# Queries and keys of chunk pairs by Strassen's seven products, in an attention block

## The chip, the cores and the metric

The kernel runs on one core of one Trainium2 chip. The metric is the device time of one execution in microseconds. The time before the change is the median of three runs, 2641.21 us (2639.83 to 2642.91).

## The reference, cut to what matters

Four sequences of 1024 tokens by 512 features are normalized (`xn`). A block of attention with 16 heads of 128 and a small product in rounded FP8 are added to the input. What the change touches is the first part: queries and local keys are products of the same tokens with two weights, and each head of them is divided by its root mean square, weighted, and rotated in its first 64 columns.

```python
q  = apply_rope(rmsnorm((xn @ Wq  + bq ).reshape(..., 16, 128), qn_w), pos)
lk = apply_rope(rmsnorm((xn @ Wlk + blk).reshape(..., 16, 128), kn_w), pos)
lv = (xn @ Wlv + blv)
# local: each chunk of 128 tokens sees itself and the chunk before it
# sparse: the 8 best of the compressed entries ck (one for 4 tokens), with values cv
out = x + ((ctx_sparse + ctx_local) * 0.5) @ Wo + bo + fp8(xn) @ fp8(input2)
```

All of it is in float32, apart from the FP8 part.

## The kernel before

The 4096 tokens are cut into 32 chunks of 128 (`t`), eight for each sequence. The 16 heads are cut into eight units of two heads (`u`). A unit of a chunk is the piece of work `n = 8 t + u`, 256 of them. One loop over slots `s` from -3 to 252 (its end is written out separately) issues, in an order written out by hand, the stages of several units: the scores of unit `s`, the queries of unit `s + 3`, the values of unit `s - 1`, the output of unit `s - 2`. No scheduler moves an instruction: each engine works through its own queue in the order of the source, and waits where data or a buffer isn't ready. All DMAs of the loop go through the SP queue, in that order too.

The stages of one unit, with the lines of the profile:

- `queries` (L606): four matmuls of 128x512 into the PSUM tile `qp` (two buffers). The 512 columns are 256 of `Wq` and 256 of `Wlk`, both heads. In chunks after the first, the first of the four inputs is `xone`, a copy of the tokens with a row of ones in it, since the bias stands in the weight's row 0.
- `squares`, `spread` (L321, L315, L316): ScalarE sums the squares of each head, GpSimd takes the power -1/2.
- `normalize` (L634): VectorE reads `qp` in PSUM and writes `th` in SBUF, four operations of 128x128. GpSimd makes one product of the rotation (L337), VectorE the other (L339, into `thb`, which is then still free) and the two sums (L341, L342).
- `turn_keys` (L687, L690, L695): VectorE transposes blocks of 32 into `thb` (one buffer), and four DMAs carry it to DRAM (`qk`). `fetch_keys` (L705) brings it back transposed as `qT` and `lkT`, two DMAs. It is called for unit `s + 2` right after the fetch of the weights in slot `s`.
- `scores` (L754, L761, L764) into `sc` (PSUM, one buffer); `weigh` (L786 to L822): VectorE masks, finds the maximum (L786) and the eight best (L807, L812), and negates the latter (L809), ScalarE takes exponentials; `settle` (L830 to L840): VectorE keeps the eight best, guards the sum (L839) and takes the reciprocal; `divide` (L847): ScalarE, four operations.
- `turn`, `fetch` (L865, L873, L907): the weights go through DRAM too: VectorE transposes blocks, one DMA writes `pr`, four read `probT`.
- `values_of` (L712): local values, four matmuls of 128x256. `values` (L924), `keep_context` (L939), `to_output` (L957): the context and its product with `wo`. All eight units' `wo` lie in SBUF for the whole run.

Beside the units, generators prepare a chunk (`chunk_prep`, `chunk_entries`, `chunk_eight`): layer norm, pooling, the FP8 part. Their steps are called at fixed units of a chunk. Their DMAs are the stores of the transposed tokens (L1091), `fetch_tokens` (L491, into `xnT`, two buffers), `fetch_with_ones` (L503), the loads of x (L105) and of angles (L111), and now and then the pooled entries (L527).

Of the order around the change, this is the heart (in slot `s`):

```python
for_unit(s, (scores, 0), (scores, 1))
for_unit(s, (weigh,))
for_unit(s + 3, (queries,))
for_unit(s + 2, (normalize,))
for_unit(s, (settle,)); for_unit(s, (divide,))
for_unit(s + 2, (go_on_rotating,), (end_rotation,))
turn(s); for_unit(s + 2, (turn_keys,))
for_unit(s - 2, (to_output,)); for_unit(s + 1, (values_of,)); for_unit(s - 1, (values,))
fetch(s); for_unit(s + 2, (fetch_keys,))
# then stores, tokens, ones and loads
```

Of the kernel before, what the change touches and what calls it, by code (L numbers as in the profile page):

```python
# [19 lines left out]
P = 128  # L20
D = 128
# [17 lines left out]
def kernel(  # L39
# [34 lines left out]
    NN = NT * NU  # L74
    assert S // RATIO <= 2 * P and NU == 8 and HID == 512
# [10 lines left out]
    def scratch(name, shape=(P, 512), dtype=F32):  # L86
        return work.tile(list(shape), dtype, tag="scratch", name=name, bufs=2)

# [19 lines left out]
    def load_angles(t):  # L108
        c = t % NCH
        cs = work.tile([P, ROPE], F32, tag="cs", name=f"cs_{t}")  # L110
        nc.sync.dma_start(cs, rope[ts(c, P), :])  # L111
        angles[t] = cs
# [10 lines left out]
    wqk_sb = [const.tile([P, KK, 512], F32, name=f"wqk_{u}") for u in range(NU)]  # L123
    wlv_sb = [const.tile([P, KK, 256], F32, name=f"wlv_{u}") for u in range(NU)]
    wo_sb = [const.tile([P, 2, HID], F32, name=f"wo_{u}") for u in range(NU)]

    def load_wqk(u, engine):
        for i, w in enumerate((Wq, Wlk)):
            engine.dma_start(
                wqk_sb[u][:, :, ts(i, 256)], w[:, ts(u, 256)].rearrange("(k p) n -> p k n", p=P)  # L130
            )
# [4 lines left out]
    def load_wo(u, engine):  # L136
        engine.dma_start(wo_sb[u], Wo[ts(u, 256), :].rearrange("(h p) n -> p h n", p=P))
# [13 lines left out]
    for k in range(KK):  # L151
        for i, w in enumerate((Wq, Wlk)):
            nc.sync.dma_start(wqk_sb[0][:, k, ts(i, 256)], w[ts(k, P), 0:256])
# [28 lines left out]
    bias_b = const.tile([P, 512], BF16, name="bias_b")  # L182
# [80 lines left out]
    def fold_first_row(u):  # L263
        w = wqk_sb[u]
        row = first_row.pop(u, None)
        if row is None:
# [3 lines left out]
                row, ident[:, 0:1].to_broadcast([P, P]), w[:, 0, :], start=True, stop=True  # L270
            )
        nc.vector.tensor_tensor(
            w, w, row.unsqueeze(1).to_broadcast([P, KK, 512]), ALU.subtract
        )
        for i, bias in enumerate((bq, blk)):
            nc.sync.dma_start(
                w[0:1, 0, ts(i, 256)], bias[ts(u, 256)].partition_broadcast(1)
            )

# [24 lines left out]
    w2_raw = [wo_sb[NU // 2 + k][:, 0, :] for k in range(KK)]  # L304

    def round_w2():
        for k in range(KK):
            spare = wo_sb[NU // 2 + k][:, 1, :]
# [14 lines left out]
    def rotate(th, cs, nh, a, name, bb=None):  # L323
# [17 lines left out]
        nc.vector.tensor_tensor(x12[:, :, 0, :], a[:, :, 0, :], bb[:, :, 1, :], ALU.subtract)  # L341
        nc.vector.tensor_tensor(x12[:, :, 1, :], a[:, :, 1, :], bb[:, :, 0, :], ALU.add)  # L342
# [135 lines left out]
    def turn_tokens_here(xt):  # L478
# [4 lines left out]
        xnT = work.tile([P, KK, P], F32, tag="xnT", name="xnT_0")  # L483
# [3 lines left out]
    def fetch_tokens(t):  # L487
        xnT = work.tile([P, KK, P], F32, tag="xnT", name=f"xnT_{t}")
# [5 lines left out]
        chunks[t] = xnT, xones[t % 2]  # L494


    xones = [const.tile([P, P], F32, name=f"xone_{i}") for i in range(2)]

    def fetch_with_ones(t):
        turned = tokens.pop(t).rearrange("i (b k) a j -> b i k (a j)", b=NB)  # L500
        for b in range(NB):
            lo = 0 if b else 1
            nc.sync.dma_start(  # L503
                xones[t % 2][b * BLK + lo : (b + 1) * BLK], turned[b, lo:, 0, :]
# [96 lines left out]
    def queries(n):  # L601
        t, u = place(n)
        xnT, xone = chunks[t]
        qp = psum.tile([P, 512], F32, tag="qp", name=f"qp_{n}")
        for k in range(KK):
            nc.tensor.matmul(  # L606
                qp,
                xnT[:, k, :] if k or not t else xone,
                wqk_sb[u][:, k, :],
# [7 lines left out]
        ss = work.tile([P, 4], F32, tag="ss", name=f"ss_{n}")  # L617
        units[n] = {"qp": qp, "ss": ss}

    def squares(n, heads):  # L620
        w = units[n]
        for i in heads:
            square_sum(w["ss"][:, i : i + 1], w["qp"][:, ts(i, D)], f"{n}_{i}")
# [5 lines left out]
    def normalize(n):  # L629
        w = units[n]  # L630
        qp, r = w.pop("qp"), w["r"]
        th = work.tile([P, 4, D], F32, tag="th", name=f"th_{n}", bufs=1)
        for i in range(4):
            nc.vector.scalar_tensor_tensor(  # L634
                th[:, i, :],
                qp[:, ts(i, D)],
# [9 lines left out]
        w["th"], w["thb"] = th, thb  # L646
# [27 lines left out]
    def key_tiles(n):  # L674
        w = units[n]
        qT = work.tile([P, NB, 2 * BLK], F32, tag="qT", name=f"qT_{n}", bufs=2)
        lkT = work.tile([P, NB, 2 * BLK], F32, tag="lkT", name=f"lkT_{n}", bufs=NU + 2)
# [3 lines left out]
    def turn_keys(n):  # L681
# [11 lines left out]
        turned = dram.tile([NB, NB, BLK, 4 * BLK], F32, tag="qk", name=f"qk_{n}")  # L693
# [43 lines left out]
    def scores(n, h):  # L737
# [6 lines left out]
        if n == NN - 2:  # L744

            w.setdefault("sc", []).append(psum.tile([P, 512], F32, tag="qp", name=f"sc_{n}_{h}"))
# [19 lines left out]
    def weigh(n):  # L766
# [5 lines left out]
            [  # L772
# [443 lines left out]
```

## Time and profile before

| what | value |
|---|---|
| median of three runs | 2641.21 us |
| profiled execution, from its first to its last instruction | 2641.7 us |
| granted TensorE clock | 0.999 |
| DMA: moved, share of 16 engines' time on the queue of the loop | 422.20 MB, 58.8% |
| qp<-wqk, L606, 128x512 float32: all 2048 instructions, busy | 968.1 us |
| vp<-wlv, L712, 128x256 float32: 2048 instructions, busy | 483.6 us |
| op<-wo, L957, 128x512 float32: 1024 instructions, busy | 481.6 us |

The profile gives each engine's busy time (PE is TensorE's matmuls, PEld its weight loads, DVE VectorE, ACT ScalarE, POOL GpSimd, SPq the SP queue that issues DMAs). A group's line has the source line, engine, operation, output and inputs, shape and count, then the busy time and the mean duration of one. Each float32 matmul call appears as two instructions. The mean duration of a matmul (593 ns at 512 columns) is longer than the time from one to the next, because they overlap in the pipeline.

### The profile page before, as it was taken

What the parts mean: (1) busy time and instruction counts of PE and PEld (TensorE: products, weight loads), DVE (VectorE), ACT (ScalarE), POOL (GpSimd) and SP (SyncE); (2) the same over time, 40 slices, a digit from 0 to 9 for tenths busy, and PEclk for the clock granted to TensorE, in tenths of its full rate; (3) what the DMA queues carried; (4) which work ended last, traced back from release to release, by engine and by line L of the source; (5) the groups of instructions that cost most, each with busy time, mean ns of one, the idle gap of its engine ahead of it and who ended that gap; (6) DMA issues with size and microseconds to landing.
All of it is one profiled execution on the core that took longest, in us unless ns stands there. A gap on an engine that the chain in (4) does not pass through costs nothing.

```text
span 2641.7 us, 46868 instructions
## 1 busy us (share of the span) xinstructions
PE 2609.3 (99%) x11879; PEld 1784.3 (68%) x11879; DVE 2213.4 (84%) x8381; ACT 1390.9 (53%) x5560; POOL 786.2 (30%) x1128
## 2 busy tenths in 40 slices
PE   8999999999999999999999999999999999999998
PEld 4666666776666666767766666667666666676776
DVE  6888888889888888888888888888888888877886
ACT  3545545555555555555555555555555555555555
POOL 3522323223332223232233322233323322322222
PEclk9999999999999999999999999999999999999999
DMA  8356556666655555666655555666665555566554
GB/s 255 110 156 162 151 145 175 171 176 158 164 143 154 162 155 156 169 173 170 166 157 144 158 149 158 177 164 164 171 176 147 150 148 153 147 168 171 159 152 110
DMA packets 722252, 422.20 MB, mean 160 GB/s; under 512 B 395823, under 2 KB 671552, under 8 KB 721984
## 3 DMA queue, kind: packets, MB, share of 16 engines
q1 hardware_dynamic: 721952, 419.20, 58.8%
q8 instruction: 97, 1.59, 0.3%
q14 instruction: 171, 1.40, 0.2%
q10 hardware_dynamic: 32, 0.02, 0.0%
HBM read 225.80 MB, written 193.20 MB: 159 GB/s over the span
## 4 chain that ended last, share of the span: by engine, by line
PE 84%; DVE 7%; ACT 3%; DMA 3%; SPq 2%; issue 1%; POOL 0%; ACTq 0%; DVEq 0%
PE qp L606 28%; PE op L957 14%; PE vp L712 14%; PE cp L924 13%; PE sc L764 5%; PE sc L761 4%; PE sc L754 4%; ACT prob L847 1%; ACT prob L814 1%; PE fp L588 1%; DVE sc L786 1%; DVE probB L865 1%; PE ep L536 1%; SPq L695 1%; DVE taken L812 1%
## 5 line engine op out<-in xcount | busy, mean ns | idle before, releaser
L606 PE MATMUL qp<-wqk,xnT 128*128 128x512 f32 x1552 | 709.8, 593 | 3.0 <-DMA wqk<-in_L_attn_Wlk_dram 2.4
L814 ACT ACTIVATE prob<-sc,neg 128x256 f32<-128x256 f32 (+1 forms) x512 | 235.9, 461 | 773.3 <-DVE taken L812 744.0
L606 PEld LDWEIGHTS qp<-wqk,xnT 128*128 128x128 f32 x1552 | 295.0, 190 | 372.5 <-issue 368.8
L847 ACT ACTIVATE prob<-prob,tot 128x256 f32<-128x256 f32 (+7 forms) x1024 | 382.0, 443 | 294.5 <-DVE tot L840 294.5
L712 PEld LDWEIGHTS vp<-wlv,xnT 128*128 128x128 f32 x2048 | 389.0, 190 | 161.3 <-issue 116.2
L957 PE MATMUL op<-wo,cT 128*128 128x512 f32 x1024 | 481.6, 593 | 4.2 <-ACT cT L939 4.2
L712 PE MATMUL vp<-wlv,xnT 128*128 128x256 f32 x2048 | 483.6, 379 | 0.0
L337 POOL TENSOR_TENSOR rb<-th,cs 128x256 f32<-128x256 f32 x256 | 203.8, 796 | 740.0 <-DVE th L634 733.2
L786 DVE CUSTOM_DVE_ANT_0 sc<-sc,mask_b 128x256 f32<-128x256 f32 (+1 forms) x512 | 211.6, 414 | 172.7 <-PE sc L764 162.7
L957 PEld LDWEIGHTS op<-wo,cT 128*128 128x128 f32 x1024 | 193.6, 190 | 229.8 <-issue 186.8
L865 DVE STREAM_TRANSPOSE probB<-prob 128x512 f32<-128x512 f32 (+2 forms) x490 | 305.8, 629 | 11.5
L315 POOL TENSOR_SCALAR r<-ss 128x4 f32<-128x4 f32 x256 | 61.9, 242 | 843.3 <-ACT junk L321 840.6
L924 PE MATMUL cp<-probT,lv 128*128 128x128 f32 x1920 | 299.0, 276 | 6.4 <-DMA probT<-pr 4.9
L321 ACT ACTIVATE junk<-qp 128x128 bf16<-128x128 f32 x1024 | 278.6, 272 | 28.9 <-PE qp L614 4.5
L924 PEld LDWEIGHTS cp<-probT,lv 128*128 128x128 f32 x1920 | 272.8, 191 | 25.4 <-issue 9.3
L634 DVE SCALAR_TENSOR_TENSOR th<-qp,r,norm_w 128x128 f32<-128x128 f32 x1024 | 286.1, 342 | 0.7 <-POOL r L316 0.4
L316 POOL TENSOR_TENSOR r<-r,nhalf 128x4 f32<-128x4 f32 x256 | 265.6, 1037 | 21.4
L830 DVE SCALAR_TENSOR_TENSOR prob<-taken,prob 128x128 f32<-128x128 bf16 (+7 forms) x512 | 186.4, 365 | 98.1 <-ACT prob L822 96.6
L606 PE MATMUL qp<-wqk,xone 128*128 128x512 f32 x496 | 258.3, 602 | 0.9 <-DMA xone<-xb_dram 0.7
L924 PE MATMUL cp<-probT,cv 128*128 128x128 f32 x1536 | 255.1, 275 | 0.0
L764 PE MATMUL sc<-ckT,qT 128*128 128x96 f32 (+7 forms) x1024 | 226.4, 303 | 0.0
L924 PEld LDWEIGHTS cp<-probT,cv 128*128 128x128 f32 x1536 | 212.7, 192 | 0.0
(141 smaller groups left out, 3674.9 us busy)
## 6 DMA issues: line engine op xcount, KB each, us to landing
pr<-probB SPq DMA_DIRECT2D x125, 512.0 KB
probT<-pr SPq DMA_DIRECT2D x500, 128.0 KB
qk<-thb SPq DMA_DIRECT2D x992, 64.0 KB
pr<-probB SPq DMA_DIRECT2D x96, 384.0 KB
probT<-pr SPq DMA_DIRECT2D x384, 96.0 KB
qT<-qk SPq DMA_DIRECT2D x248, 128.0 KB
lkT<-qk SPq DMA_DIRECT2D x248, 128.0 KB
x_norm<-_attn_hidden_states_dram SPq DMA_DIRECT2D x32, 256.0 KB
```

The lines of the kernel that those rows point to most:

```text
L316: nc.gpsimd.tensor_tensor(r, r, nhalf[: ss.shape[0], 0:n], ALU.pow)
L321: nc.scalar.activation(junk[: src.shape[0]], src, AF.Square, accum_out=acc)
L606: nc.tensor.matmul(qp, xnT[:, k, :] if k or not t else xone, wqk_sb[u][:, k, :], start=(k == 0), stop=(t > 0 and k == KK - 1),)
L634: nc.vector.scalar_tensor_tensor(th[:, i, :], qp[:, ts(i, D)], r[:, i : i + 1], norm_w[:, i // 2, :], ALU.mult, ALU.mult,)
L712: nc.tensor.matmul(vp[:, 0:256], xnT[:, k, :], wlv_sb[u][:, k, :], start=(k == 0), stop=(k == KK - 1),)
L764: nc.tensor.matmul(sc[:, spa], q, ckT[:, 0:m], start=True, stop=True)
L786: nc.vector.tensor_tensor_reduce(sc[h][:, loc], sc[h][:, loc], mask_b[:, loc], -1.0, TAKEN, ALU.add, ALU.min, neg[h][0],)
L814: nc.scalar.activation(probs[h][:, loc], sc[h][:, loc], AF.Exp, bias=neg[h][0], scale=-1.0, accum_out=tot[:, h, 0:1],)
L847: nc.scalar.mul(probs[h][:, cols], probs[h][:, cols], tot[:, h, part : part + 1])
L865: nc.vector.transpose(pb[:, :, ds(h * g, g), :], prob[:, parts[0] * P : (parts[-1] + 1) * P].rearrange("p (g b i) -> p b g i", b=NB, i=BLK),)
L924: nc.tensor.matmul(blocks(cp[:, h, :]), v, probT[:, :, h * len(parts) + i - parts[0], :], start=(i == parts[0]), stop=(i == parts[-1]),)
L957: nc.tensor.matmul(op, cT[:, h, :], wo_sb[u][:, h, :], start=(u == 0 and h == 0), stop=(u == NU - 1 and h == 1),)
```

## The change

Queries and keys of two neighbouring chunks (2p and 2p + 1) are computed together for units of chunks 4 to 31 (`FIRST` = 32 is the first such unit). The product of the two chunks' tokens (two halves of the 512 features) with the unit's weights (the same halves of the features by the two blocks of 256 columns, `Wq` and `Wlk`) is a 2x2 block product. Strassen's algorithm, in the form with shared sums, makes it by seven block products instead of eight. Each of the seven (`p1` to `p7`) is two matmul calls of 128x256.

- The sums of tokens are made once for a pair of chunks (`sum_tokens`, four GpSimd operations of 128x256). In the weights, one block is replaced once by a combination (`combine_weights`, two GpSimd operations for a unit, in slots 23 to 30); three further differences are made anew for each pair of units (`sum_weights`, one GpSimd operation of 128x512 each, into two buffers).
- Partial products accumulate in two PSUM banks (`qk_banks`). ScalarE copies an intermediate stand into `th` (`keep1`, `keep6`, `keep5`, `keep3`), and VectorE adds the other bank to it (`sum2`, `sum7`, `sum4`). `normalize` then reads `th` in SBUF instead of PSUM.
- The first eight pairs are made in slots 29 to 36, one whole pair a slot ("both"), and both units are then normalized, rotated and transposed one after the other in the next slot, ahead of `settle`. After that a pair takes two slots: "one" makes p1, p2, p6, p7, "two" makes p5, p3, p4; the first unit of a chunk pair begins eleven slots before its use. The two units are normalized in the two slots that follow. The last pair is made in slots 243 and 244.
- The order of the units stays. The results wait in DRAM (`qk`, now 24 buffers). `fetch_keys` is now called for unit `s + 1` directly after the scores in slot `s`. `lkT` has nine buffers instead of ten.
- To make room, only two of the eight `wo` tiles stay in SBUF (units 0 and 4). The other six are loaded for every chunk anew into two buffers, 512 KB each, at the end of a slot. Tokens have four buffers with the ones' row in the same tile.
- The two sums of the rotation move from VectorE to GpSimd. One negation does for both heads, and the guard of the sum is left out except in the first chunk of a sequence.

The diff, cut to its core:

```diff
+    def combine_weights(u):
+        (b11, b12), (_, b22) = ([flat(wqk_sb[u][:, j, i]) for i in range(2)] for j in range(2))
+        nc.gpsimd.tensor_tensor(b12, b12, b11, ALU.subtract)
+        nc.gpsimd.tensor_tensor(b12, b22, b12, ALU.subtract)
+
+    def sum_weights(q, which):
+        w = wqk_sb[q % NU]
+        a, b, to = {
+            1: (w[:, 1, 1], w[:, 0, 1], 1),
+            3: (w[:, 0, 1], w[:, 0, 0], 0),
+            4: (w[:, 1, 0], w[:, 0, 1], 0),
+        }[which]
+        nc.gpsimd.tensor_tensor(flat(weight_sums[to]), flat(a), flat(b), ALU.subtract)
...
+        adder = nc.gpsimd if nh > 1 else nc.vector
+        adder.tensor_tensor(x12[:, :, 0, :], a[:, :, 0, :], bb[:, :, 1, :], ALU.subtract)
+        adder.tensor_tensor(x12[:, :, 1, :], a[:, :, 1, :], bb[:, :, 0, :], ALU.add)
...
+    def product(i, a, b, first=True):
+        for k in range(2):
+            nc.tensor.matmul(
+                regions[i],
+                a[k],
+                b[:, k, :],
+                start=first and k == 0,
+                stop=k == 1,
+                skip_group_check=not first,
+            )
...
+    def p6(q):
+        product(0, both(token_sums[1]), wqk_sb[q % NU][:, 0, 1], False)
+    def keep6(q):
+        take_th(q, 1)
+        nc.scalar.copy(half(q, 1, 0), regions[0])
+    def p7(q):
+        product(1, both(token_sums[2]), weight_sums[0])
+    def sum7(q):
+        add_to(half(q, 1, 1), 1)
...
+    def add_to(v, i):
+        nc.vector.tensor_tensor(v, v, regions[i], ALU.add)
```

The order in a slot after the change (`what` is "one", "two" or "both"):

```diff
         for_unit(s, (scores, 0), (scores, 1))
+        if s + 1 >= NU:
+            for_unit(s + 1, (fetch_keys,))
+        if what in ("one", "both"):
+            sum_weights(q, 3)
+        if what == "both" or q == FIRST // 2 + NU:
+            sum_weights(q, 1)
+        if what == "two":
+            sum_weights(q, 4)
         for_unit(s - 2, (keep_context,))
+        if s in last_sum_at:
+            sum4(last_sum_at[s])
+        if what in ("one", "both"):
+            p1(q)
+            keep1(q)
+            if s > FIRST - 3:
+                p2(q)
+        elif what == "two":
+            p5(q)
+            keep5(q)
+            if q + 1 < NN // 2:
+                sum_weights(q + 1, 1)
         for_unit(s, (weigh,))
...
+        if what == "two":
+            sum7(q)
+        for n in jobs:
+            normalize(n)
+            if len(jobs) > 1:
+                go_on_rotating(n)
+                end_rotation(n)
+                turn_keys(n)
+        for_unit(s - 2, (to_output,))
+        if what in ("one", "both"):
+            p6(q)
         for_unit(s, (settle,))
+        if what in ("one", "both"):
+            sum2(q)
         for_unit(s, (divide,))
+        if len(jobs) == 1:
+            go_on_rotating(jobs[0])
+            end_rotation(jobs[0])
         if by_dma(s):
             turn(s)
+        if len(jobs) == 1 and jobs[0] >= NU:
+            turn_keys(jobs[0])
+        if what in ("one", "both"):
+            keep6(q)
...
+        for_unit(s + 1, (values_of,))
+        if what in ("one", "both"):
+            p7(q)
+        if what == "two":
+            p3(q)
+            keep3(q)
+            p4(q)
+        if what == "both":
+            sum_weights(q, 4)
+            p5(q)
+            keep5(q)
...
         for_unit(s - 1, (values,))
+        if what == "both":
+            p3(q)
+            keep3(q)
+            sum7(q)
+            p4(q)
+            sum4(q)
...
         if by_dma(s):
             fetch(s)
-        if s + 2 >= NU:
-            for_unit(s + 2, (fetch_keys,))
...
+        load_wo_for(s)
```

## The prediction

> **What bounds the kernel now.** I read the busy shares first, then the windows by stretch, then the groups, then one late step in order of time (columns: start us, duration us, engine, instruction).
>
> ```profile
> PE 2609.3 (99%) x11879; PEld 1784.3 (68%) x11879; DVE 2213.4 (84%) x8381; ACT 1390.9 (53%) x5560; POOL 786.2 (30%) x1128
> ```
> ```profile
> 0.00:342.00 342.00, 320.80 (x1389) 210.47 (x1390) 273.57 (x1044) 165.65 (x694) 119.65 (x182) 0.99 0.59 165
> 342.00:426.00 84.00, 81.66 (x378) 55.98 (x377) 71.43 (x273) 46.15 (x187) 25.06 (x38) 1.00 0.62 164
> 426.00:2574.00 2148.00, 2146.20 (x9809) 1474.21 (x9808) 1822.72 (x6901) 1144.69 (x4565) 626.78 (x891) 1.00 0.60 160
> 2574.00:2641.00 67.00, 60.67 (x307) 43.66 (x306) 45.64 (x165) 34.41 (x116) 14.68 (x17) 1.00 0.42 114
> ```
> From 426 us on, TensorE is busy in 2146.2 of 2148.0 us at granted clock 1.00: it sets the pace of every slot, and nothing else waits long. A slot (one unit) lasts 8.72 us in the first chunk of a batch and 9.63, 9.63, 9.63, 10.15, 10.26, 10.37, 10.48 in the next seven (medians, from the first score matmul of one slot to that of the next).
>
> What hides under TensorE, and how closely, decides this change:
>
> ```profile
> 1298.57 0.34 SPq L873 DMA_DIRECT2D pr<-probB  x1
> ...
> 1299.22 1.92 SPq L695 DMA_DIRECT2D qk<-thb  x4
> ...
> 1301.30 1.75 SPq L907 DMA_DIRECT2D probT<-pr  x4
> ...
> 1303.22 0.38 SPq L705 DMA_DIRECT2D qT<-qk  x1
> ...
> 1303.64 0.51 SPq L705 DMA_DIRECT2D lkT<-qk  x1
> ...
> 1304.19 1.90 SPq L491 DMA_DIRECT2D xnT<-xb_dram  x4
> ...
> 1306.22 0.18 DVE L840 RECIPROCAL tot<-tot 128x4 f32<-128x4 f32 x1
> ```
> This slot's first score matmul starts at 1298.27, the next slot's at 1308.75. The SP queue issues a DMA each 0.4 to 0.6 us. The keys (qT, lkT) go out 4.65 us after pr and must have landed two slots after the slot that pr belongs to. By the trace's landing events (issue to last increment, medians) pr takes 2.66 us at 512 KB (1.98 at 256 KB), qk 1.83, probT 2.67, qT and lkT 2.98. The keys are there before the score matmuls by 1.7, 2.8, 2.7, 2.2, 2.3, 2.3, 2.0, 1.5 us in chunks 0 to 7 of a batch. That small margin is the number to remember.
>
> **The change part by part.**
>
> *TensorE.* The matmul rows count two instructions per call. Weight loads of L606 stand 0.43 us apart at 512 columns; eight of L712 (256 columns) fill 1.89 us, 0.216 each. A pair of units now costs 2 x 8 x 0.429 = 6.86 us; seven products of two calls, 28 x 0.216, cost 6.05. That is 0.82 less for each of 112 pairs, 92 us at most. A slot "one" (p1, p2, p6, p7) keeps its length (+0.03), a slot "two" (p5, p3, p4) loses 0.86.
>
> *VectorE, each unit.* Out: the two rotation adds, 0.51 of a slot (0.292 + 0.284 by duration); L839 for all but the first chunk, 0.21; one of two L809, about 0.1. In: three 128x256 adds per pair by the row of kv<-ep,bkv_sb (397 ns), 0.6 per unit. So VectorE gets about 0.2 lighter; normalizing from SBUF I leave at L634's price (342 ns; the row of the same shape with SBUF inputs, kv<-kv,er,norm_w, shows 314).
>
> *GpSimd.* In per pair: three weight sums of 128x512 (rows 1.26 to 1.34 us, so 3.8) and four rotation adds. Rows of 728 ns at 128x256 and 1.26 us at 128x512 give 2.1 ns a column and 0.19 fixed, so 0.46 each as an estimate. Busy about 5.5 of 10 us, enough.
>
> *ScalarE.* Four copies of 128x256 per pair (366 ns): 1.5 us on an engine that is busy 53%. Hidden.
>
> *A price that the busy times don't show.*
>
> ```profile
> L839 DVE TENSOR_SCALAR tot<-tot x256: 169/170/1186, 34.1 to 2630.6; 128x4 f32<-128x4 f32 x128
> ```
> Minimum, median and maximum: 170 ns, but 51 of them over 900. Each of those starts while a GpSimd operation of 128x512 is in flight (L294, L298) and ends 25 ns after it. The added weight sums put three such operations into each pair, so a VectorE instruction can lose up to 1.3 us to one. In steady slots the sums run while VectorE works from PSUM (weigh): I take 0; the upper end is 3.8 per pair.
> [...]
>
> *Eight dense slots (29 to 36), where one slot makes a whole pair.* Here TensorE would need 2.6 more per slot, but the chain is longer. From a slot's first score matmul in chunk 4, by before's rows: scores end 1.5, weigh ends 4.5, normalize 5.6, the two rotation products 6.8, GpSimd's adds 7.8, transposes to thb 8.5. Four qk issues (the last at 10.0) land at 11.9. thb is one buffer, and the second unit's rotation writes it: it waits for that landing, because VectorE's order has both units ahead of settle. Rotation 12.4, adds 13.4, transposes 14.2, settle 15.1, reciprocal 15.3, sum2 15.8. p7 overwrites the bank that sum2 reads: 16.7. ScalarE's four divides and keep6 end at 17.5, p5 18.4, values 20.1, p3 21.0, p4 (sum7 is done at 19.3) 21.9. So 21.9 where there were 9.6 to 10.2. GpSimd has the power of two units and two weight sums ahead of the first rotation, about 0.6 more: 22.5. Seven such slots add 7 x 12.4 = 87. Slot 29 (p2 behind normalize, sum7 behind chunk work) adds about 6, slot 37, which still normalizes two units, 7. **Together +100**; 60 if the second rotation waited for nothing (adds overlapping settle), 120 with GpSimd blocking.
>
> *Steady slots 38 to 244, the SP queue.* The keys of slot s+1 are now issued at the top of slot s, which in the queue is behind the stores, tokens, ones and x loads that used to follow them, and behind a new 512 KB wo load in six of eight slots. A wo costs 0.51 to issue; the rings' time is bounded by pr (128 KB more takes 0.33, so 1.3 for 512 KB) and by x_norm against cs (2.97 against 2.64 for 224 KB more, so 0.7), of which about 0.4 passes while qT is issued. I take pr's: 1.4 in all. Two slots are 0.84 shorter and pr comes 0.2 earlier, so the margins become 1.7 - 0.84 + 0.2 - 1.4 and so on: -0.3, 0.75, 0.65, 0.15, 0.25, 0.25, -0.05, -0.55; mean 0.15. Whatever else stands ahead of the keys is paid by TensorE. By before's issue spacing (stores 0.67, tokens 0.48, ones 0.45, pooled 0.55, fewT 0.52, x loads 0.5), in 16 slots: tokens 1.9, then tokens, ones, cs, x_sum without wo 3.2, then pooled, ones, cs, x_norm 3.6 (of neighbours, each stall counts against the next: 1.75 + 1.35 + 2.1); stores 2.7 twice (2.55 each); pooled and x_norm 1.1, with fewT each fourth chunk 3.7 (1.6). Sum 11.9, times 13: 155. The shortened slots give 104 x 0.84 = 87. **Net +67.** With 0.7 for the rings +30; hidden entirely, -87; with 2 us for the rings +120.
>
> *p7 behind sum2 in slots "one".* Reciprocal ends 5.4 to 8.05 after the slot's start in chunks 0 to 7; less 0.3, plus 0.5 for sum2, against p7's natural 6.03 after the scores: late only in chunks 6 and 7, by 0.2 and 0.4, more behind chunk work: 26 in all if the keys don't stall TensorE first. I take 0, as they do.
>
> *The rest.* Slots 9 to 28 have the later keys but no shorter slot: 3 to 4 us a chunk, +10. The last eight slots lose 3.43 us of TensorE work each, but the key loop (reciprocal, pr, probT, keys) holds them near 9.5 to 10: -5. L839's 51 blocked executions (0.94 each) lay mostly under TensorE: 0.
>
> Sum against the profiled execution's 2641.7 (the median of the runs is 2641.2, the same): 2641.7 + 100 + 67 + 10 - 5 = **2814**; I say 2805, the ring estimate being on the high side.
>
> **The rivals.**
> - *Keys in time, dense slots as above.* If a wo doesn't hold up the DMAs behind it and the queue drains in the waits, the 87 is kept but for p7's 26: 2641.7 + 100 - 87 + 26 - 15 = 2665. For it: 58.8% of DMA time, so rings are idle. Against it: margins of 1.5 to 2.8 us and eight SP issues of half a microsecond.
> - *GpSimd becomes the brake.* If its sums drift under normalize and settle, VectorE loses up to 3.8 per pair, of which about 1.2 of slack hides: 104 x 2.6 = 270 at most, of which a third comes on top of the key stalls: about 2900. For it: L839's 1110 ns. Against it: the order puts sums under weigh.
> - *Faster.* One mechanism: the dense slots stay TensorE-bound (12.8 each, which is in the 92 already) and the keys are hidden: 2641.7 - 92 + 26 = 2576. It decides if the second rotation needn't wait for the qk landings; from dense slots of about 18 us on, with the keys hidden, it is no longer faster.
> - *That it doesn't do what it says* (28 matmuls of 256 columns): only if these ran slower than L712's 0.216, which the like shape excludes.
>
> **How the numbers follow.** Forecast 2805 with 0.60 (2700 to 2870); keys in time 0.20 (2645 to 2700); GpSimd 0.14 (2870 to 2950); faster 0.04; within 0.2% of now (about what a measurement of this kernel can tell from no change) 0.02. Slower 0.94. The range, 2660 to 2890, takes the forecast, most of the second case and the nearest part of the third.
>
> **What would show it.** Slots 30 to 36 of about 22 us, with L417 waiting for qk landings and p7 for sum2. After that, TensorE's first score matmul waiting for lkT, in the slots after stores and tokens, for 1 to 3 us; TensorE busy near 90%. I am wrong if dense slots last 13 to 16 us, if no wait for lkT shows, or if normalize's duration doubles under the weight sums.

## The result, and the profile after

The changed kernel takes 3002.06 us (median of four runs, 2998.32 to 3005.07) against 2640.74 of the kernel before on the same chip: a ratio of 1.1366, 95% interval 1.135 to 1.1382. The profiled execution spans 2999.1 us. The forecast was 2805, with a range up to 2890; the direction was right, the size was not.

First the busy times of the changed kernel (engine, busy us, share of the span, instructions).

```profile
PE 2662.2 (89%) x13188; PEld 2085.5 (70%) x13223; DVE 2339.8 (78%) x7736; ACT 1568.5 (52%) x6008; POOL 1475.5 (49%) x2049
```

TensorE was busy 99% of the time and now stands still for a tenth of it. Its busy time did not fall with its work (2609.3 us before): the profile models the ends of matmuls, so a matmul that starts late or runs slowly can still count as busy. Next the windows of the changed kernel: slots -3 to 28, the dense slots 29 to 37, the steady slots 38 to 244, and the end (columns: window, length, busy us of PE, PEld, DVE, ACT, POOL, then the granted clock, DMA share, GB/s).

```profile
0.00:369.00 369.00, 328.08 (x1365) 216.66 (x1371) 263.43 (x941) 167.53 (x694) 158.85 (x256) 0.95 0.63 176
369.00:587.00 218.00, 138.35 (x601) 110.22 (x603) 124.83 (x352) 75.05 (x299) 103.44 (x138) 0.81 0.36 101
588.00:2880.00 2292.00, 2098.68 (x10734) 1683.46 (x10758) 1885.36 (x6214) 1272.32 (x4850) 1195.05 (x1635) 0.99 0.64 181
2880.00:2999.00 119.00, 96.12 (x486) 74.21 (x488) 66.13 (x231) 53.56 (x167) 17.16 (x20) 0.94 0.52 155
```

By the first score matmul of each slot, the time went here:

| stretch | before | after | difference | predicted |
|---|---|---|---|---|
| start and slots 0 to 7 | 117.0 | 119.6 | +2.6 | 0 |
| slots 8 to 28 | 220.5 | 249.9 | +29.4 | +10 |
| dense slots, 29 to 37 | 98.2 | 218.3 | +120.1 | +100 |
| steady slots, 38 to 244 | 2085.0 | 2292.2 | +207.2 | +67 |
| slots 245 to the end | 120.9 | 119.2 | -1.7 | -5 |

The steady slots hold the larger part of the miss, 140 us of it. What TensorE waited for, over the whole changed kernel (us in total, times, longest):

```profile
PE qk L699 <- DVE th L778: 133.8, 99, 11.0
PE sc L914 <- DMA qT<-qk: 49.8, 45, 6.1
PE op L1112 <- ACT cT L1094: 37.0, 58, 1.8
PE sc L921 <- DMA lkT<-qk: 25.6, 28, 2.9
PE sc L914 <- ACT cT L1094: 25.4, 11, 5.3
```

The keys (qT, lkT) are late, as forecast: 75 us by name. Some 45 us more of waits at the two score lines (L914, L921) are put down to ScalarE's steps, such as the 25.4 above; with the keys fetched first (e2) under 5 us of waits are left at these lines, so most of these belong to the keys too. Beside them stands the wait of a product for one of VectorE's additions (L778: sum2, sum4, sum7): 74 us in the dense slots, where the prediction had it, and 60 in the steady ones, where it had set it to nought. In the steady slots alone the keys cost TensorE more waiting, some 95 us:

```profile
PE qk L699 <- DVE th L778: 59.7, 90, 2.3
PE sc L914 <- DMA qT<-qk: 32.1, 37, 3.1
```

A late key, in the queue of DMA issues of the changed kernel (start, duration, queue, line, DMA) and in TensorE's instructions behind it:

```profile
1459.72 0.38 SPq L1342 DMA_DIRECT2D pooled<-xb  x1
1460.14 1.61 SPq L579 DMA_DIRECT2D tokens<-xb_dram  x4
1461.79 0.42 SPq L160 DMA_DIRECT2D wo<-in_L_attn_Wo_dram  x1
1462.32 0.41 SPq L117 DMA_DIRECT2D cs<-in_rope_dram  x1
1462.77 0.43 SPq L111 DMA_DIRECT2D x_norm<-_attn_hidden_states_dram  x1
1463.25 0.43 SPq L865 DMA_DIRECT2D qT<-qk  x1
...
1467.02 0.47 PE L914 MATMUL sc<-lkT,qT 128*128 128x128 f32 x2 [1.55 <-DMA qT<-qk]
```

Eight issues stand ahead of qT and take 3.5 us; TensorE, ready before 1465.5, gets its operand at 1467.0.

And the blocked VectorE, in another steady slot of the changed kernel:

```profile
1483.72 1.31 POOL L333 TENSOR_TENSOR weight_sum<-wqk 128x512 f32<-128x512 f32 x1
...
1484.03 1.94 DVE L794 SCALAR_TENSOR_TENSOR th<-th,r,norm_w 128x128 f32<-128x128 f32 x4
...
1486.05 0.81 POOL L415 TENSOR_TENSOR rb<-th,cs 128x256 f32<-128x256 f32 x1 [1.02 <-DVE th L794]
...
1486.20 0.91 DVE L984 SCALAR_TENSOR_TENSOR prob<-taken,prob 128x224 f32<-128x224 bf16 x1
```

The first of normalize's four pieces starts at 1484.03, while the weight sum runs until 1485.03, and the four take 1.94 us instead of 1.1; the second settle operation starts beside GpSimd's product of the rotation and takes 0.91 instead of 0.38. Over the kernel, 135 pieces of L794 started while a weight sum ran: median 1136 ns. The line's own summary (minimum, median, maximum in ns) shows what a median hides:

```profile
L794 DVE SCALAR_TENSOR_TENSOR th<-th,r,norm_w x884: 308/344/1494, 395.4 to 2895.7; 128x128 f32<-128x128 f32 x177
```

A second operation is held up too: the negation that the change made for both heads at once (L966, 128x2). In the kernel before it was two operations of 128x1. As many subtractions put into that kernel (run e9, below) leave them as they are, at 156 ns at most; first e9, then the changed kernel:

```profile
L813 DVE TENSOR_SCALAR neg<-top x512: 153/154/156, 31.0 to 2626.0; 128x1 f32<-128x1 f32 x171
```
```profile
L966 DVE TENSOR_SCALAR neg_spa<-top x256: 158/160/1306, 31.1 to 2985.5; 128x2 f32<-128x2 f32 x128
```

### The profile page after: what moved, and what is told of

It is laid out like the page before. It is cut to its first block, busy times and chain, and to the rows that moved or that the text cites. A ratio compares the mean times of both kernels' runs of the same rounds, so it can differ in the third digit from the quotient of the medians.

```text
span 2999.1 us, 50657 instructions
## 1 busy us (share of the span) xinstructions
PE 2662.2 (89%) x13188; PEld 2085.5 (70%) x13223; DVE 2339.8 (78%) x7736; ACT 1568.5 (52%) x6008; POOL 1475.5 (49%) x2049
## 4 chain that ended last, share of the span: by engine, by line
DVE 30%; PE 24%; DMA 10%; ACT 8%; SPq 6%; issue 6%; POOL 2%; DVEq 0%; ACTq 0%; POOLq 0%
PE qk L699 7%; DVE th L794 5%; ACT prob L1002 5%; PE cp L1079 4%; DVE prob L984 4%; DVE sc L943 4%; DMA qT<-qk 3%; DVE taken L965 3%; DMA lkT<-qk 3%; PE op L1112 3%; DVE top L964 3%; PE sc L924 3%; PE sc L921 2%; PE vp L872 2%; SPq L1062 2%
## 5 line engine op out<-in xcount | busy, mean ns | idle before, releaser
L872 PE MATMUL vp<-wlv,tokens 128*128 128x256 f32 x2048 | 483.6, 379 | 0.0
L872 PEld LDWEIGHTS vp<-wlv,tokens 128*128 128x128 f32 x2048 | 389.4, 190 | 102.5 <-issue 51.4
L333 POOL TENSOR_TENSOR weight_sum<-wqk 128x512 f32<-128x512 f32 x337 | 430.2, 1291 | 41.6 <-PE qk L699 41.3
L943 DVE CUSTOM_DVE_ANT_0 sc<-sc,mask_b 128x256 f32<-128x256 f32 (+1 forms) x510 | 210.6, 413 | 275.0 <-PE sc L924 265.7
L794 DVE SCALAR_TENSOR_TENSOR th<-th,r,norm_w 128x128 f32<-128x128 f32 x884 | 367.7, 476 | 0.3
L699 PE MATMUL qk<-weight_sum,token_sums 128*128 128x256 f32 x896 | 251.9, 408 | 106.1 <-DVE th L778 105.0
L399 ACT ACTIVATE junk<-th 128x128 bf16<-128x128 f32 x884 | 273.8, 310 | 21.2
L914 PE MATMUL sc<-lkT,qT 128*128 128x128 f32 x892 | 192.6, 299 | 92.7 <-DMA qT<-qk 49.8
L699 PEld LDWEIGHTS qk<-weight_sum,token_sums 128*128 128x128 f32 x896 | 168.0, 201 | 151.1 <-issue 89.6
L699 PE MATMUL qk<-wqk,tokens 128*128 128x256 f32 x896 | 240.7, 404 | 32.0 <-DVE th L778 28.6
L420 POOL TENSOR_TENSOR th<-thb,rb 128x128 f32<-128x128 f32 x253 | 116.2, 459 | 291.3 <-DVE thb L417 286.8
```

The costliest lines, as they stand in the source:

```text
L333: nc.gpsimd.tensor_tensor(flat(weight_sums[to]), flat(a), flat(b), ALU.subtract)
L399: nc.scalar.activation(junk[: src.shape[0]], src, AF.Square, accum_out=acc)
L699: nc.tensor.matmul(regions[i], a[k], b[:, k, :], start=first and k == 0, stop=k == 1, skip_group_check=not first,)
L794: nc.vector.scalar_tensor_tensor(th[:, i, :], qp[:, i, :], r[:, i : i + 1], norm_w[:, i // 2, :], ALU.mult, ALU.mult,)
L872: nc.tensor.matmul(vp[:, 0:256], xnT[:, k, :], wlv_sb[u][:, k, :], start=(k == 0), stop=(k == KK - 1),)
L943: nc.vector.tensor_tensor_reduce(sc[h][:, loc], sc[h][:, loc], mask_b[:, loc], -1.0, TAKEN, ALU.add, ALU.min, neg[h],)
```

## The experiments

Theories: **1**, GpSimd's weight sums hold up VectorE (predicted at 0, upper end 3.8 us a pair). **2**, the keys are late in the SP queue (predicted at 155 us). **3 to 5**, a place in an engine's order makes one product late. **6**, VectorE as a whole becomes the brake.

### Each of the two causes by itself

e1, weight sums later in the slot:

```diff
-        if what == "two":
-            sum_weights(q, 4)
...
             p7(q)
+        if what == "one":
+            sum_weights(q, 4)
...
             p4(q)
+            sum_weights(q + 1, 3)
+            sum_weights(q + 1, 1)
```

> The three weight sums of a pair are issued on GpSimd later in the slot: in a slot "one" the sum for p4 right behind p7, in a slot "two" the two sums of the next pair right behind p4, each ahead of the power for the norm. GpSimd then runs them while VectorE transposes and works from PSUM. Theory 1 (weight sums hold up VectorE's operations on SBUF, sum2 comes late, p7 waits): the waits of TensorE for sum2 (134 us in all, about 15 of them in the dense slots) mostly go, slots "one" fall from a mean of 11.5 us to about 10.5, and the time falls by 90 to 130 us, to 2870 to 2910. Theory 2 (keys late in the SP queue): within 25 us of 3002, since the queue is not touched. Theory 1 is wrong if normalize still lasts 1 us behind a sum in a hundred places and the time stays; if normalize is undisturbed and the time still stays, the waits go over to the keys.

e2, keys ahead of the other DMAs (`loads_of_slot` holds stores, tokens, ones, wo and angles of the slot before):

```diff
         if s + 1 >= NU:
             for_unit(s + 1, (fetch_keys,))
+        if u == 3 and 0 <= t < NT:
+            load_x(t, "sum")
...
+        loads_of_slot(s - 1)
```

> All stores, token, ones, angle and wo loads of a slot's end, the x loads and the loads of pooled entries at a slot's start are issued behind the two fetches of keys of the next slot, so that nothing but qk, pr and probT stands ahead of the keys. Theory 2 (keys late in the SP queue, as predicted with 155 us): TensorE's waits for qT and lkT (75 us in all) go, and the time falls by 75 to 155 us, to 2850 to 2925. Theory 1 (weight sums): the waits for keys go, but the slots are held by sum2 as well, so that at most half shows, 2950 to 3000.

e3 makes both edits.

> The two edits before together: weight sums later in the slot, and keys ahead of all other DMAs. If the two causes are separate and both real, the gains add or more than add (each hides part of the other): 2750 to 2830, which is the dense slots' 120 us, the 29 us of slots 9 to 28 and little else above the time before. If a third cause holds the steady slots, it stays above 2850.

e4 leaves the sums out (plain blocks of the weights stand in their place, so the products are not Strassen's any more):

```diff
-        nc.gpsimd.tensor_tensor(flat(weight_sums[to]), flat(a), flat(b), ALU.subtract)
+        plain[to] = a
...
-        product(1, both(token_sums[2]), weight_sums[0])
+        product(1, both(token_sums[2]), plain[0])
```

> Left out of the computation: the three weight sums of each pair; p7, p4 and p5 take plain weight blocks in their place. All else is as in the changed kernel, the DMA queue too. Theory 1: at least what the later sums give, 2850 to 2900, with normalize at 314 to 345 ns throughout and sum2 in time; what it gives beyond the later sums is what these still cost. Theory 2: within 30 us of 3002.

e8 joins e2 and e4.

> Left out of the computation: the three weight sums of each pair (plain blocks in their place). The keys are fetched first as in e2. If sums and keys are two separate causes whose prices add: 3002 less 93 less 111, about 2798. If they hide one another (a slot waits for the later of the two), less than that is left: 2740 to 2780. If they are the same time counted twice, 2830 to 2890.

| run | us | ratio to before, 95% interval | steady slots | VectorE busy in them |
|---|---|---|---|---|
| changed kernel | 3002.1 | 1.135 to 1.1382 | 2292.2 | 1885.4 |
| e1, sums later | 2978.7 | 1.126 to 1.1298 | 2277.6 | 1813.4 |
| e2, keys first | 2909.4 | 1.1001 to 1.1034 | 2214.2 | 1926.9 |
| e3, both | 2872.0 | 1.0858 to 1.0891 | 2178.5 | 1830.4 |
| e4, no sums | 2890.7 | 1.0934 to 1.0967 | 2201.5 | 1727.5 |
| e8, no sums, keys first | 2765.0 | 1.0456 to 1.0487 | 2087.3 | 1734.9 |

Both causes are real. Keys first gives 93 us, no sums 111, both 237: more than the sum, as it must be where a slot waits for the later of the two. Moving the sums (e1) missed its expectation: normalize waits for the power behind them (32 us of waits for `r`), and the waits for qT grow from 50 to 71 us. With both edits, e3 stayed above its 2750 to 2830, so the two edits leave something. VectorE's column is the price of the sums: 158 us from e4 to the changed kernel, and moving the sums takes off less than half. Of the 158, normalize has 99 (333.1 us busy in the steady slots against 234.3 in e4), the negation L966 55 (95.5 against 40.1) and settle (L984) 4. VectorE hardly waited for GpSimd's results there: of its waits in the steady slots only the 31.8 us of the layer norm (`off`) are for GpSimd, with 0.2 beside.

e11, is it the wo loads that delay the keys?

```diff
             wo_of[n] = wo_sb[i]
-            load_wo(n % NU, wo_sb[i], nc.sync)
+            if s < 8:
+                load_wo(n % NU, wo_sb[i], nc.sync)
```

> Left out of the computation: from slot 8 on the wo tiles of units 1 to 3 and 5 to 7 are not loaded again, so that the output takes whichever weights lie in the buffer. All else is as in the changed kernel. If the 512 KB loads are the larger part of what holds the keys (prediction: 1.4 us each, some 80 of the 155 us): 2915 to 2960. If the keys are late because of the stores, tokens, ones and x loads ahead of them: within 25 us of 3002.

2978.3 us (1.1261 to 1.1294), 24 less (this kernel then uses whatever `wo` lies in the buffer): mostly not. e10 then put the keys' late place alone into the kernel before:

```diff
         for_unit(s, (scores, 0), (scores, 1))
+        if s + 1 >= NU:
+            for_unit(s + 1, (fetch_keys,))
...
-        if s + 2 >= NU:
-            for_unit(s + 2, (fetch_keys,))
```

> The kernel before, with one part of the change alone: the keys of unit s + 1 fetched directly after the scores of slot s, behind stores, tokens, ones and x loads, instead of those of unit s + 2 at the end of slot s. No wo loads, no Strassen. By the prediction's price for slots 9 to 28 (3 to 4 us a chunk for late keys without wo loads), 28 chunks cost 80 to 115 us: 2720 to 2755. If the margin of about 2 us swallows what stands ahead of the keys without wo loads: 2641 to 2660, and the price in the changed kernel comes from the wo loads and the shorter slots.

2718.6 us (1.027 to 1.0304), 78 more, just under the expected 80 to 115. TensorE's waits over this whole kernel:

```profile
PE sc L754 <- DMA qT<-qk: 34.0, 18, 5.2
PE sc L761 <- DMA lkT<-qk: 10.3, 17, 1.7
```

44 us of named waits stand for 78 us of time. A wait is counted from the modelled end of the matmul before, which is later than the next could have started: from start to start, the score matmuls of slots 8 to 244 lost some 59 us. The rest is the clock: by the trace's clock rows TensorE ran at half clock for 55 us of these slots (none in the kernel before), which cost it some 20, an estimate from the matmuls that started at twice their usual spacing.

### Is it the order, or VectorE as a whole?

e5 (on e3) and e6 (on the changed kernel) take sum2 from behind settle to directly behind weigh:

```diff
         for_unit(s, (weigh,))
+        if what in ("one", "both") and s > FIRST - 3:
+            sum2(q)
```

> The sums later and the keys first, as in e3, and sum2 on VectorE directly behind weigh instead of behind settle (from slot 30 on). Theory 3 (p7 waits because sum2 stands behind normalize and settle in VectorE's order, whatever makes these late): the 71 us that TensorE still waits for sum2 in the steady slots go, and the dense slots lose about 1 us each: 2785 to 2815. Theory 1 (only the blocking by GpSimd matters): sum2 early hides nothing else, VectorE is as late as before and the wait goes to the next step of the slot: 2850 to 2872.

> The changed kernel with one thing altered: sum2 directly behind weigh. Theory 3 (order of sum2) as a cause of its own: the waits of TensorE for sum2 go and the time falls by 60 to 100 us, 2900 to 2940. If the keys hold the same slots, the waits go over to qT and lkT, as they did when the sums were moved alone (31 to 48 us for qT): 2960 to 2990.

e5: 2885.3 us (1.0914 to 1.095), 13 more than e3. e6: 3034.1 (1.1473 to 1.1507), 32 more than the changed kernel. Both lie above every range that was expected. Theory 3 falls. The waits for the additions shrank (in the steady slots from 74 us in e3 to 24 in e5), and those of the output for ScalarE's cT rose from 34 to 77; half clock in the steady slots rose too, from 31 us to 51.

e7 sets the dense slots' second unit apart, on e5:

```diff
-        for n in jobs:
+        for n in jobs[:1]:
             normalize(n)
...
             turn(s)
+        for n in jobs[1:]:
+            normalize(n)
+            go_on_rotating(n)
+            end_rotation(n)
+            turn_keys(n)
```

> As e5, and in the eight dense slots the second unit's normalize, rotation and transposes come behind settle and the transposes of the weights, so that the wait of its rotation for the landing of the first unit's qk lies under other work. If that chain sets the dense slots (as predicted), they fall from 24 us to 15 to 17: e5 less 55 to 75 us, 2715 to 2755. If TensorE at its clock of 0.81 sets them, they fall by less than 3 us each: e5 less 20 at most.

2839.3 us (1.0739 to 1.0771), 46 less than e5; slots 30 to 36 fall from 181.9 to 142.3 us, from 26.0 a slot to 20.3. So that chain is a part of it, and the clock alone (under 3 us a slot) is refuted; but the 15 to 17 us expected were missed, and of the some 15 us by which e5's dense slot is longer than one before, 5.7 went. No run parts the rest.

e12 puts the output behind the values (on e3, with e7's dense slots); e13, on e12, also moves the values of the next unit forward and p2 and p7 back in slots "one":

```diff
-        for_unit(s - 2, (to_output,))
...
         for_unit(s + 1, (values_of,))
+        for_unit(s - 2, (to_output,))
```

```diff
+        if what == "one":
+            values_of(s + 1)
+            p2(q)
...
         for_unit(s - 1, (values,))
+        if what == "one":
+            p7(q)
+            sum_weights(q, 4)
```

> The sums later and the keys first as in e3, the second unit of the dense slots behind settle as in e7, sum2 at its old place, and the output of unit s - 2 on TensorE behind the values of unit s + 1 instead of directly behind p2 or p5 (before the change it stood late in the slot too). From e3's 2872: the dense slots give 46 (e7 against e5). Theory 4 (the output, moved ahead, waits for ScalarE's cT, which stands behind the squares at the slot's end: 35 us of waits in e3, 75 in e5): 30 us more, 2785 to 2800. If those waits only go over to p6 and p7: 2815 to 2835.

> As e12, and on TensorE in slots "one" the values of unit s + 1 and then p2 come behind normalize in the order, p7 behind the values of unit s - 1 at the slot's end, with the sum for p4 behind it. In e12, p2 waits 61 us for sum4 of the pair before and p7 53 us for sum2, and slots "two" already stand at TensorE's pace (9.45). Theory 5 (the steady slots lose only where a product overwrites the bank that VectorE has still to read, so it is a matter of where p2 and p7 stand): these 114 us mostly go, 2715 to 2750. Theory 6 (VectorE, with what GpSimd blocks, is itself the brake; the waits are only where it shows): they go over to other places, 2790 to 2825.

e14 is e13 without the sums, e15 the changed kernel with only the altered order.

> As e13, with the three weight sums of each pair left out of the computation. By theory 5 the sums cost something only through p2 and p7: within 30 us of e13, of which about 10 in the dense slots. By theory 6, VectorE is freed of what GpSimd blocks (95 us of its time in e3) and the time falls by 60 us or more against e13.

> The changed kernel with only TensorE's order altered: output behind the values, p2 and p7 later in slots "one", the sums, the keys and the dense slots as they were. If the waits on VectorE and ScalarE are a cause beside the keys: 60 to 110 us less, 2890 to 2940. If the late keys take their place, as when the sums alone were moved (e1): 2950 to 2995.

e12: 2822.1 us (1.0672 to 1.0703), so the cT waits went over. e13: 2842.7 (1.0749 to 1.0785), 21 more than e12 and above both of its ranges. e15: 3002.9 (1.1353 to 1.1387), nothing, which neither range had: the waits for the additions went, but those for keys and for probT rose, and its steady slots ran at half clock for 116 us instead of 62. e14: 2736.0 (1.0348 to 1.038), 107 less than e13. Theories 4 and 5 fall. 6 fits best: whatever the order, the loss shows at what TensorE needs next, and most of it goes when the sums go. The same view of waits, first e12, then e13:

```profile
PE qk L699 <- DVE th L778: 109.1, 92, 2.7
PE cp L1079 <- DMA probT<-pr: 29.9, 16, 5.3
```
```profile
PE cp L1079 <- DMA probT<-pr: 88.6, 81, 4.7
PE qk L699 <- DVE th L778: 25.7, 32, 3.2
```

In e13 the additions are mostly in time, and the weights' way (VectorE's transposes, pr, probT) is late instead. That wait isn't the sums' alone: from 620 to 2500 us it is 57.6 us in e13 and still 51.5 in e14, so e13's order has a price of its own.

### Why the sums are dear here

e9 adds as many GpSimd subtractions to the kernel before, written in bfloat16 to a tile that nothing uses any more:

```diff
+    def sum_weights(q, to):
+        w = wqk_sb[q % NU]
+        nc.gpsimd.tensor_tensor(bias_b, w[:, 2 * to, :], w[:, 2 * to + 1, :], ALU.subtract)
...
         for_unit(s, (scores, 0), (scores, 1))
+        if 37 <= s < 245:
+            sum_weights(s // 2, 0)
...
+        if 37 <= s < 245 and s % 2 == 0:
+            sum_weights(s // 2, 1)
```

> The kernel before, with 312 GpSimd subtractions of 128x512 added at the places that the weight sums have in the changed kernel (slots 37 to 244, three in two slots); nothing uses their results, which are written in bfloat16 into a tile no longer needed. Theory 1 in its strong form (an operation of VectorE that is held up costs its time wherever it stands): the 158 us of VectorE time that the sums add in the changed kernel show in the time, 2740 to 2800. In its weak form (before, TensorE covers VectorE by about 1.5 us a slot, and only sum2 ahead of p7 puts VectorE on TensorE's path): VectorE's busy time grows by 100 to 160 us, but the time stays within 2641 to 2680.

2643.5 us (1.0 to 1.0019): nothing. VectorE's busy time in the steady slots grew by 60 us (1768.9 to 1829.1), less than the 100 to 160 expected, and under TensorE's cover. But normalize was not held up at all. In e9 its 362 pieces that started beside a sum took 342 ns. They read PSUM there. e16 moves normalize's input to SBUF, e17 adds the sums to that:

```diff
+            for i in range(2):
+                nc.scalar.copy(th[:, ts(i, 256)], qp[:, ts(i, 256)])
...
+            th = w["th"]
+            qp = th.rearrange("p h d -> p (h d)")
```

> The kernel before, with normalize's input moved to SBUF as in the changed kernel, for units after the eighth: ScalarE copies the queries' PSUM tile to th behind the squares (two copies of 128x256), and VectorE normalizes th in place. It is the base for e17. The copies wait for the transposes of the unit before (th is one buffer), and ScalarE has half of its time free: 2641 to 2700, with normalize at 340 to 360 ns a piece.

> As e16, with the 312 GpSimd subtractions of e9. In e9 they cost 2 us, and normalize, which read PSUM there, kept 342 ns beside them; in the changed kernel, where it reads SBUF, 135 of its operations that began beside a sum lasted 1136 ns. If the place of normalize's input is what makes the sums dear: normalize's mean goes up by 80 ns or more against e16, VectorE's busy time in the steady slots by 60 us more than the 60 of e9, and the time by 30 us or more. If the sums are dear only through the add-ups of Strassen's products: within 10 us of e16.

e16: 2646.0 us (1.0001 to 1.002). e17: 2687.5 (1.0152 to 1.0183). The groups of normalize (count, then busy us and mean ns of one), in e9, e16 and e17:

```profile
L638 DVE SCALAR_TENSOR_TENSOR th<-qp,r,norm_w 128x128 f32<-128x128 f32 x1024 | 286.3, 343 | 2.7 <-POOL r L316 2.4
```
```profile
L648 DVE SCALAR_TENSOR_TENSOR th<-th,r,norm_w 128x128 f32<-128x128 f32 x988 | 282.1, 348 | 1.3 <-POOL r L316 0.7
```
```profile
L652 DVE SCALAR_TENSOR_TENSOR th<-th,r,norm_w 128x128 f32<-128x128 f32 x988 | 417.9, 483 | 3.1 <-POOL r L316 2.8
```

Sums alone cost 2 us, SBUF input alone 3, both 44. VectorE's busy time in the steady slots is 1779.1 in e16 and 1928.7 in e17, 150 more where e9 had 60 more. So the place of normalize's input makes it one that sums can hold up. In the changed kernel, whose slots "two" are shorter and whose negation is held up besides, the sums cost 111.

## Why the prediction was wrong, point by point

- **The step that failed:** "In steady slots the sums run while VectorE works from PSUM (weigh): I take 0; the upper end is 3.8 per pair." VectorE's time grew by 158 us over 104 pairs, 1.5 a pair, and with it the time by 91 us of the steady slots (e4), or 127 once the keys are in time (e2 to e8). The sums did not stay under weigh: in the steady slots 117 of 310 run directly behind GpSimd's power, 93 behind another sum and 77 behind the FP8 steps, and they reach the negation and normalize. The row for it was in the prediction (L839, 170 ns or 1186); that normalize, once it reads SBUF, can be held up too, e9 against e17 shows (a mean of 343 ns with the sums in e9, 483 in e17). What was wrong is the place of the sums in time, from which the 0 came; that weigh keeps its time beside a sum it showed by no row, but it came true (L943, 432 ns). The rival that GpSimd becomes the brake, at "about 2900" and 0.14, has this mechanism, and the prediction's own sign, that normalize's duration doubles under the sums, came: 1136 ns where the median of all is 344. Not seen was the negation, counted as a saving of about 0.1 a slot: made one for both heads it took 743 ns beside a sum instead of 159, and has 55 of the 158 us. "p7 behind sum2 ... I take 0" failed with it: 60 us of waits for the additions in the steady slots, though altering that order gained nothing (e5, e6, e13).
- **The miss of 140 us in the steady slots, by terms:** without sums and late keys (e8) they take 2087, so the shorter slots, -87, gave nothing: 89. Late keys then add 114 (e8 to e4) where 155 stood: -41. The sums add 91 (e4 to the changed kernel) where 0 stood. In the other order keys and sums come to 78 and 127. So a second term was as wrong as the sums, the shorter slots.
- **Keys, +155 in the steady slots:** mechanism right, size too high. Keys first gives 78 us there, 114 without the sums. Alone in the kernel before, late keys cost 78 in all (e10), 58 in the steady slots. The 1.4 us for each wo load was too much: without them the whole kernel is 24 us faster (e11).
- **Shorter slots "two", -87:** the price was right where nothing else waits. In e12 the median slot "two" of chunks 1 to 3 lasts 8.79 us against 9.63, 0.84 less (9.29 in e8). But with keys and sums both removed (e8) the steady slots take 2087, not 2085 less 87: of these 89 us, 55 are named waits (cT 24.5, the additions 11.3, probT 10.2, wo 6.5, others 3). Counted from one matmul's start to the next, the named waits come to some 70, and half clock to 5; the rest stays unattributed. Of these waits the prediction had a term only for that of p7 for sum2, at 0.
- **Dense slots, +100, measured +120:** the chain was the forecast one. In slot 31 of the changed kernel:

```profile
420.38 3.23 DVE L794 SCALAR_TENSOR_TENSOR th<-th,r,norm_w 128x128 f32<-128x128 f32 x4
420.44 0.47 ACT L968 ACTIVATE prob<-sc,neg 128x256 f32<-128x256 f32 x1
420.63 2.58 POOL L333 TENSOR_TENSOR weight_sum<-wqk 128x512 f32<-128x512 f32 x2
...
429.70 0.43 DVE L417 TENSOR_TENSOR thb<-tokens,cs 128x256 f32<-128x256 f32 x1 [2.28 <-DMA qk<-thb]
...
432.86 0.39 DVE L778 TENSOR_TENSOR th<-th,qk 128x256 f32<-128x256 f32 x1
...
433.40 3.75 PE L699 MATMUL qk<-weight_sum,token_sums 128*128 128x256 f32 x8 [8.96 <-DVE th L778]
```

  The second rotation waits 2.28 us for the landing of qk, and p7 waits 8.96 us for sum2. Two terms were too small: normalize took 3.23 us beside two weight sums instead of 1.1 (without the sums, e4, the nine slots are 12 us shorter), and after the pause the next eight matmuls started 427 ns apart instead of 216. That is 1.7 us in this slot; in the nine slots, matmuls at half clock took some 17 us longer, an estimate made as for e10.
- **Slots 8 to 28, +10, measured +29:** the same late keys. Keys first takes back 21 us, no wo loads 8; late keys alone cost 16 in the kernel before (e10). Part of it is the clock, 0.94 there in the changed kernel and 0.99 with the keys first (e2).
- **The clock, which the prediction left at 1 throughout:** its mean is 0.968 in the changed kernel and 0.999 before. By the trace's clock rows TensorE ran at half clock for 193 us of the changed kernel (8 before): 82 in the dense slots, 62 in the steady ones, 31 in slots 8 to 28. Matmuls at half clock took some 60 us longer by the same estimate, 27 of them in the steady slots. This is no third cause, since it comes with the pauses (in the steady slots each of the 17 stretches of half clock lies next to a pause of 1.7 to 3.2 us), but it is a price on top of them: without late keys the steady slots have 24 us of half clock (e2), without the sums too 10 (e8).
- **VectorE 0.2 lighter a unit:** right without the sums (1727.5 against 1768.9 in 207 slots, 0.2 each).
- **The rival "keys in time", 2665**, is refuted as a whole: with keys first the time is 2909.
- No experiment on the changed kernel beat the kernel before. The best that leaves nothing out is e12, at 1.07 of its time.

## What to carry to other kernels

When a change moves an operand from PSUM to SBUF, or makes one operation of two, ask of that instruction what it can newly collide with, and not only how long it takes alone (here, beside a sum, normalize took 342 ns from PSUM and 1136 from SBUF, the negation 154 at 128x1 and 743 at 128x2); and ask when the other one will really run, not only where it stands in the source. An added load on an idle engine is cheap or dear by what runs beside it: the same 312 GpSimd operations cost 2 us or 42. A wait of TensorE can cost more than its length, if the granted clock drops with it: after the pause of 8.96 us matmuls started 427 ns apart instead of 216. And where two late things share a slot, each experiment by itself shows less than its price; if waits move when the order is altered and the sum stays, look for the engine behind them, not for the next place in the order.

## What the runs showed of the hardware

- A VectorE operation with two SBUF operands (L794, 128x128), started beside a 128x512 GpSimd subtraction, lasted 1136 ns (median of 135), where the median of all is 344; the same with one operand in PSUM (e9, L638) 342. A tensor_scalar of only 128x2 (L966) lasted 743 ns (median of 93) instead of 159 and ended 24 ns after the GpSimd operation; of 128x1 (e9, L813) it kept its 154 ns beside one (146 times). No run alters that shape alone. The PSUM reads of weigh (L943, 432 ns) kept their time beside a sum, and so did the block transposes (in e3, L847, 404 ns, 120 times).
- The granted clock was 0.81 in the dense slots, where TensorE was busy least (138 of 218 us), and 0.89 there in e7 (136 of 179). After the pause of 8.96 us the matmuls ran at half pace for about 4 us (128x256 at 427 ns until 436.9, context matmuls at 213 until 437.6, then 112 and 216).
- By the clock rows of the changed kernel's trace, the half clock of that pause began at 427.4 us, 3.0 us into it, and ended at 437.6, 4.2 us behind it. In the steady slots the longest pause of TensorE (start to start, less the usual spacing) is 3.2 us; the clock rows show 17 stretches of half clock there, each next to a pause of 1.7 to 3.2 us, while 70 pauses of 1 to 3 us have none. So a pause of 1.7 us came with half clock, and one of 3.0 without.
